# A four-layer graph network on one core: the first group's rows fetched into idle product buffers, and its half blocks projected two at a time amid the first queries

## The chip, the cores and the metric

The kernel runs on one core of a Trainium2 chip. The metric is device time of one execution, in microseconds (us); smaller is better. Before the change it is 3035.61 us, the median of three runs.

## The reference

The input x has 16 graphs of 1024 nodes with 128 features each; one random adjacency matrix (1024 x 1024, about 8 neighbours per node) serves all graphs. Four layers follow one another: L0, L2 and L3 are multi-head attention over neighbours with a feed-forward part, L1 is a graph attention layer. Cut to what matters:

```python
# L0, L2, L3 (8 heads of 16)
Q, K, V = h @ Wq, h @ Wk, h @ Wv
scores = where(adj == 0, -inf, Q K^T / sqrt(16))
x = layer_norm(h + softmax(scores) V @ Wo + bo)
out = layer_norm(x + relu(x @ W1 + b1) @ W2 + b2)
# L1
h = x @ W;  e = leaky_relu(h @ a_src [i] + h @ a_dst [j]), masked by adj
out = layer_norm(softmax(e) h + x)
```

## The kernel before

**Layout.** Nodes are sorted by degree first (the setup, up to about 154 us of the profile), so that a block of 128 sorted nodes has a known bound on neighbours. The 16 graphs are cut into two groups (g) of 8, a group into two halves (h) of 4. There are T = 8 node blocks (t). A *half block* is one (g, t, h): 128 nodes of 4 graphs, 128 x 512 floats, 256 KB.

**Projection.** For every layer and group a table in DRAM holds keys and values of all nodes (1024 rows of 8 KB in attention layers). `project` (L362) takes a half block turned to features x nodes (tile xT): it writes it to DRAM on SP's queue (`kept`, L364), multiplies it with Wkv in two pairs of matmuls (L371), copies each from PSUM to the tile kv on ACT (L375), and writes kv into the table on SP's queue (L380). kv lies in the pool `twos`, which has two buffers for each tag. `turned` (L425) makes xT: four PE transposes (L429) and a copy on ACT (L431). xT has two buffers.

**First layer's input.** `first(g)` (L512) does this for all 16 half blocks of a group: an indirect DMA on POOL's queue gathers the rows in sorted order into the tile xg (L517, one buffer), then come `turned` and `project`. It is a generator: each `yield` ends one step.

**Units.** A unit is one (layer, g, t). Its neighbours come in parts: `gathered` (L581) fetches up to two table rows per node by indirect DMA on POOL (tile e, four buffers, L591), three parts ahead. On DVE, `products` (L597) multiplies them with the queries (L600), `exponentials` (L604) reduces (L614), and ACT takes the exponential (L618); `weighted` (L628) multiplies the values with it (L639), one part later. The products lie in the tile pr, four buffers. `summed` adds them over neighbours on PE (acc, L666). `queries(u)` (L551) needs the unit's x, loaded from `kept` by `loaded(u)` (L540): Wq matmuls (L566), a copy q (L570), replication on PE (L575), copies qr (L578). At the end of a unit `divided` takes the reciprocal (L687), and two tails (`attention_tail`) do the rest of the layer and project for the next one: output projection (L465, L466), norm (L413 and L422 on ACT, L419 on POOL), feed-forward (L479, L483, L488), and again `project`. Unit 0 has ten parts, units 1 to 3 have six each, units 4 to 7 four each, and the same in every group and layer.

**Order.** The order of instructions on each engine is the order in which the program issues them (`manual_schedule`). The main loop goes over all parts of all units. Between the steps of a part `others()` (L713) is called three times: it advances tails, paced over the unit, and then either `fronts` (the next unit's queries) or, where there are none, `slow`:

```python
        if fronts:
            advance(fronts)
        elif slow:
            advance(slow)
```

In an attention part two of these calls stand between the weighted products and the exponentials, and one after the sums; no main work lies between the first two except at a unit's turn. Ahead of the main loop (L723 to L730) `first(0)` is run to its end, x of units 0 and 1 is loaded, and `queries(0)` is run to its end. `first(1)` becomes `slow`: group 1 is projected beside the first units of group 0, a step at a time. It needs three calls for a half block: one for the table write of the half block before, the gather and `turned`, and one for each pair of projections.

Of the kernel before, what the change touches and what calls it, by code (L numbers as in the profile page):

```python
# [12 lines left out]
F32 = mybir.dt.float32  # L13
# [7 lines left out]
P = 128  # L21
D = 128
# [19 lines left out]
T = N // P  # L42
GR = 2
G = B // GR
HF = 2
GH = G // HF
# [30 lines left out]
def sparse_path(ctx: ExitStack, tc: tile.TileContext, a: dict, out: bass.AP, flag):  # L77
# [257 lines left out]
    reps = ctx.enter_context(tc.tile_pool(name="reps", bufs=2))  # L335
    ones_ = ctx.enter_context(tc.tile_pool(name="ones_", bufs=1))
    twos = ctx.enter_context(tc.tile_pool(name="twos", bufs=2))
    smalls = ctx.enter_context(tc.tile_pool(name="smalls", bufs=3))
    exps = ctx.enter_context(tc.tile_pool(name="exps", bufs=2))

    def gather_buffer():
# [17 lines left out]
    srcs = {}  # L359


    def project(l, g, t, h, x):  # L362

        nc.sync.dma_start(kept[l, g][t, :, h, :], x.rearrange("p g n -> p (g n)"))  # L364
        table = tables[l, g][t * P : (t + 1) * P, :]
        if LAYERS[l][1] is ATTN:
            kv = twos.tile([P, 2, GH, D], F32, tag="kv", name="kv")
            for i in range(0, GH, 2):
                ps = bank([P, 2, 2 * D])
                for k in range(2):  # L370
                    nc.tensor.matmul(  # L371
                        ps[:, k, :], x[:, i + k, :], w[LAYERS[l][0], "Wkv"],
                        start=True, stop=True,
                    )
                nc.scalar.copy(  # L375
                    kv[:, :, i : i + 2, :].rearrange("p c g d -> p g c d"),
                    ps.rearrange("p g (c d) -> p g c d", d=D),
                )
                yield
            nc.sync.dma_start(  # L380
                table.rearrange("p (c x) -> p c x", c=2)[:, :, h * GH * D : (h + 1) * GH * D],
                kv.rearrange("p c g d -> p c (g d)"),
            )
            return
        kv = twos.tile([P, GH * D + GH], F32, tag="kv", name="kv")
        if h == 0:
            srcs[g, t] = const.tile([P, G], F32, name=f"src{g}{t}")
        for i in range(0, GH, 2):
            ps = bank([P, 2, D + 2])
            for k in range(2):  # L390
                nc.tensor.matmul(ps[:, k, :], x[:, i + k, :], wg, start=True, stop=True)
            nc.scalar.copy(
                kv[:, i * D : (i + 2) * D].rearrange("p (g d) -> p g d", d=D), ps[:, :, :D]
            )
            to = GH * D + i
            nc.scalar.copy(
                kv[:, to : to + 2].rearrange("p (g o) -> p g o", o=1), ps[:, :, D : D + 1]
            )
            at = h * GH + i
            nc.scalar.copy(  # L400
                srcs[g, t][:, at : at + 2].rearrange("p (g o) -> p g o", o=1), ps[:, :, D + 1 :]
            )
            yield

        nc.sync.dma_start(table[:, h * GH * D : (h + 1) * GH * D], kv[:, : GH * D])
        nc.sync.dma_start(table[:, ROW + h * GH : ROW + (h + 1) * GH], kv[:, GH * D :])
# [18 lines left out]
    def turned(z, dst, gain=None, shift=None):  # L425

        ps = bank([P, GH, P])
        for i in range(GH):
            nc.tensor.transpose(ps[:, i, :], z[:, i, :], ident)  # L429
        if gain is None:  # L430
            nc.scalar.copy(dst, ps)  # L431
        else:
            nc.scalar.activation(dst, ps, AF.Identity, bias=shift, scale=gain)  # L433
# [75 lines left out]
        yield  # L509
        yield from finish(l, g, t, h, z, w["L1", "ln_gamma"], w["L1", "ln_beta"])  # L510

    def first(g):  # L512

        for t in range(T):
            for h in range(HF):
                xg = ones_.tile([P, GH, D], F32, tag="xg", name="xg")
                nc.gpsimd.indirect_dma_start(  # L517
                    out=xg.rearrange("p g d -> p (g d)"), out_offset=None,
                    in_=a["x"].rearrange("n (k c) -> (n k) c", k=GR * HF),
                    in_offset=bass.IndirectOffsetOnAxis(ap=places[:, g, h, t : t + 1], axis=0),  # L520
                )
                xn = states.tile([P, GH, P], F32, tag="xT", name="xT")
                turned(xg, xn)
                yield
                yield from project(0, g, t, h, xn)


    units = [(l, g, t) for l in range(len(LAYERS)) for g in range(GR) for t in range(T)]
# [11 lines left out]
    def loaded(u):  # L540

        if u >= len(units):
            return
        l, g, t = units[u]
        xs[units[u]] = inputs.tile([P, HF, GH, P], F32, tag="x", name="x")
        nc.sync.dma_start(
            xs[units[u]].rearrange("p h g n -> p (h g n)"),
            kept[l, g][t].rearrange("p h c -> p (h c)"),
        )

    def queries(u):  # L551

        l, g, t = units[u]
        if not is_attention(u):
            ps = bank([P, J, G])
            for j in range(J):
                nc.tensor.matmul(ps[:, j, :], rep_of(j, True), srcs[g, t], start=True, stop=True)
            ofs[u] = smalls.tile([P, J, G], F32, tag="of", name="of")
            nc.scalar.copy(ofs[u], ps)
            return  # L560
        qs[u] = reps.tile([P, J, ROW], F32, tag="qr", name="qr")
        for h in range(HF):
            q = ones_.tile([P, GH * D], F32, tag="q", name="q")
            ps = bank([P, GH, D])
            for i in range(GH):
                nc.tensor.matmul(  # L566
                    ps[:, i, :], xs[l, g, t][:, h, i, :], w[LAYERS[l][0], "Wq"],
                    start=True, stop=True,
                )
            nc.scalar.copy(q, ps.rearrange("p g d -> p (g d)"))  # L570
            yield
            pss = []
            for j in range(J):
                ps = bank([P, GH * D])
                nc.tensor.matmul(ps, rep_of(j), q[32 * j : 32 * j + 32], start=True, stop=True)  # L575
                pss.append(ps)
            for j in range(J):
                nc.scalar.copy(qs[u][:, j, h * GH * D : (h + 1) * GH * D], pss[j])  # L578
            yield
# [141 lines left out]
            advance(slow)  # L721

    with tc.manual_schedule():  # L723
        for _ in first(0):
            pass
        loaded(0)
        loaded(1)
        for _ in queries(0):
            pass
        slow.append(first(1))  # L730
        for i in range(AHEAD):
            gathered(i)
        closing = None
        begun = 0
        for i in range(len(parts) + 1):
            here = i < len(parts)
            u = parts[i][0] if here else len(units)
            if here:
                l = units[u][0]
                if i and parts[i - 1][0] != u:  # L740
                    begun = i
                    if units[u][1:] == (0, 1) and l + 1 < len(LAYERS):
                        if LAYERS[l + 1][1] is ATTN:
                            load_weights(LAYERS[l + 1][0])
                if is_attention(u):
                    products(i)
                else:
                    exponentials(i)
            ends = i + 1 >= len(parts) or parts[i + 1][0] != u
            if i:  # L750
                weighted(i - 1, 0)
                if not is_attention(parts[i - 1][0]):
                    others()
                    weighted(i - 1, 2)
                gathered(i - 1 + AHEAD)
            others()
            if closing is not None:
                while tails:
                    advance(tails)
                for _ in closing:  # L760
                    pass
                closing = None
                passes = 3 if is_attention(u) else 4
                steps = STEPS if is_attention(parts[begun - 1][0]) else GRAPH_STEPS
                pace[:] = 0.0, steps / (passes * sum(part[0] == u for part in parts) - 1)
            if here and u + 1 < len(units):
                if i == begun + 1:
                    loaded(u + 2)
                    fronts.append(queries(u + 1))
            others()  # L770
            if here and is_attention(u):
                exponentials(i)
            if i:
                summed(i - 1)
                if parts[i - 1][0] != u:
                    closing = divided(parts[i - 1][0])
                    next(closing)
            others()
            if ends:

                while fronts:
                    advance(fronts)
        while tails:
            advance(tails)
        for _ in closing:
            pass
        while tails:
            advance(tails)
# [434 lines left out]
```

## Time and profile before

| | us |
|---|---|
| median of three runs | 3035.61 (3032.30 to 3037.83) |
| the profiled execution | 3036.25 |
| its span | 3034.5 |
| mean granted PE clock | 0.846 |

| engine | busy us | share of the span |
|---|---|---|
| PE (matmul) | 2124.9 | 70% |
| PEld (weight load) | 1325.2 | 44% |
| DVE | 2150.0 | 71% |
| ACT | 1424.2 | 47% |
| POOL | 1478.1 | 49% |

The DMA queues moved 615 MB, 203 GB/s over the span. The shares are means over stages that differ: the setup with DVE's sorting, the projection of group 0, then 64 units. For a change in one stage the busy time and the waits of that stage count. The time of the profiled execution stands 1.75 us above its span, and 0.64 us above the median.

### The profile page before, as it was taken

The numbers are of one execution on the slowest core, as the hardware profiler recorded it, in microseconds if no ns is written. First come the engines' busy times: TensorE is split into PE (matmuls) and PEld (weight loads), VectorE is DVE, ScalarE is ACT, GpSimd is POOL, SyncE is SP. The second block draws the span as 40 slices with busy tenths as digits, with TensorE's granted clock in tenths as the row PEclk, the third lists the DMA queues.
The fourth block names the chain that finished last, engine by engine and source line by source line (L and its number), as shares of the span: only waits on it lengthen the run. The fifth ranks groups of instructions, "written<-read, shape, count | busy, mean of one in ns | idle before, by whom it ended". The sixth has DMA issues, their size and how long they took to land.

```text
span 3034.5 us, 35305 instructions
## 1 busy us (share of the span) xinstructions
PE 2124.9 (70%) x12569; PEld 1325.2 (44%) x12569; DVE 2150.0 (71%) x1493; ACT 1424.2 (47%) x4468; POOL 1478.1 (49%) x1086
## 2 busy tenths in 40 slices
PE   1365767776777786766577887777877676766766
PEld 1343444543554443434245554555544444334444
DVE  7505768768887666675798767887678877778772
ACT  1033445563556544435345664456543555334454
POOL 0123435443444568685335443354435577466673
PEclk9986888887888888988788988889887888787887
DMA  1057766545555468777665654656546553355540
GB/s 56 12 181 287 304 215 236 204 169 217 223 225 179 171 210 288 256 272 282 221 238 216 228 205 179 271 218 230 200 183 245 198 216 145 144 219 210 195 144 22
DMA packets 171144, 615.36 MB, mean 203 GB/s; under 512 B 44472, under 2 KB 47928, under 8 KB 122462
## 3 DMA queue, kind: packets, MB, share of 16 engines
q0 software_dynamic: 99584, 480.93, 43.4%
q1 hardware_dynamic: 71376, 132.10, 11.9%
q8 instruction: 101, 1.65, 0.2%
q14 instruction: 83, 0.68, 0.1%
HBM read 650.67 MB, written 100.73 MB: 248 GB/s over the span
## 4 chain that ended last, share of the span: by engine, by line
PE 40%; DVE 15%; ACT 14%; POOL 11%; issue 10%; DMA 8%; another core or an unknown queue 0%; SPq 0%; POOLq 0%; DVEq 0%; ACTq 0%
PE ps L479 7%; PE yps L488 6%; PE ps L429 5%; ACT z L413 5%; POOL e L591 5%; PE acc L666 5%; POOL rstd L419 4%; DVE sc L614 4%; DMA xg<-in_x,places 3%; DVE pr L639 3%; PE ps L371 3%; DVE pr L600 3%; ACT qr L578 3%; PE yps L465 3%; PE yps L492 3%
## 5 line engine op out<-in xcount | busy, mean ns | idle before, releaser
L591 POOL DMA_INDIRECT e<-table,idx x656 | 886.1, 1351 | 448.1 <-DVE pr L639 263.4
L639 DVE TENSOR_TENSOR pr<-e,ex 128x2048 f32<-128x2048 f32 (+1 forms) x344 | 760.1, 2216 | 338.7 <-ACT ex L618 333.4
L419 POOL TENSOR_TENSOR rstd<-total,power 128x4 f32<-128x4 f32 x224 | 359.9, 1608 | 753.4 <-ACT z L413 718.9
L600 DVE TENSOR_TENSOR pr<-e,qr 128x2048 f32<-128x2048 f32 (+1 forms) x258 | 565.1, 2190 | 195.1 <-ACT qr L578 138.1
L666 PE MATMUL acc<-pr,marks 128*32 128x512 f32 x2624 | 467.7, 701 | 146.5 <-DVE pr L639 136.6
L614 DVE TENSOR_REDUCE sc<-pr 128x128 f32<-128x2048 f32 (+1 forms) x258 | 561.9, 2178 | 0.0
L429 PE MATMUL ps<-ident,z 128*128 128x128 f32 x768 | 199.4, 368 | 246.5 <-ACT z L422 246.5
L429 PEld LDWEIGHTS ps<-ident,z 128*128 128x128 f32 x768 | 126.5, 172 | 396.2 <-ACT z L422 325.7
L371 PE MATMUL ps<-Wkv,xT 128*128 128x256 f32 x768 | 244.5, 466 | 41.5 <-ACT xT L431 21.2
L479 PE MATMUL ps<-x,W 128*128 128x512 f32 x384 | 241.1, 761 | 41.8 <-ACT x L433 41.8
L488 PE MATMUL yps<-W,f 128*128 128x128 f32 x1536 | 258.5, 287 | 13.0 <-ACT f L483 11.0
L666 PEld LDWEIGHTS acc<-pr,marks 128*32 128x32 f32 x2624 | 89.4, 120 | 398.5 <-issue 213.8
L488 PEld LDWEIGHTS yps<-W,f 128*128 128x128 f32 x1536 | 212.5, 197 | 69.9 <-ACT f L483 44.3
L483 ACT ACTIVATE f<-ps,b 128x512 f32<-128x512 f32 x192 | 131.4, 687 | 230.8 <-PE ps L479 230.0
L578 ACT COPY qr<-ps 128x512 f32<-128x512 f32 x384 | 197.6, 596 | 74.9 <-PE ps L575 74.7
L413 ACT ACTIVATE z<-y,root 128x128 f32<-128x128 f32 x512 | 198.5, 396 | 50.6 <-DVE y L506 35.4
L575 PE MATMUL ps<-q,rep 32*128 32x512 f32 x768 | 169.7, 679 | 67.4 <-ACT oT L431 41.3
L371 PEld LDWEIGHTS ps<-Wkv,xT 128*128 128x128 f32 x768 | 166.2, 231 | 91.2 <-ACT xT L431 29.3
L618 ACT ACTIVATE ex<-sc 128x128 f32<-128x128 f32 (+1 forms) x258 | 81.1, 314 | 253.6 <-DVE sc L614 236.1
L465 PE MATMUL yps<-Wo,oT 128*128 128x128 f32 x768 | 180.2, 322 | 7.5 <-ACT oT L431 6.9
L375 ACT COPY kv<-ps 128x512 f32<-128x512 f32 x192 | 112.5, 587 | 140.9 <-PE ps L371 129.4
L413 ACT ACTIVATE z<-yps,root 128x128 f32<-128x128 f32 x384 | 135.6, 368 | 77.2 <-PE yps L492 77.2
(128 smaller groups left out, 2977.8 us busy)
## 6 DMA issues: line engine op xcount, KB each, us to landing
table<-kv SPq DMA_DIRECT2D x96, 512.0 KB
kept<-xT SPq DMA_DIRECT2D x128, 256.0 KB
x<-kept SPq DMA_DIRECT2D x64, 512.0 KB
e<-table,idx POOLq DMA_INDIRECT x656
table<-kv SPq DMA_DIRECT2D x32, 256.0 KB
edges<-in_adj SPq DMA_DIRECT2D x8, 512.0 KB
W<-in_L_gnn_W SPq DMA_DIRECT2D x6, 128.0 KB
xg<-in_x,places POOLq DMA_INDIRECT x32
```

The lines of the kernel that those rows point to most:

```text
L371: nc.tensor.matmul(ps[:, k, :], x[:, i + k, :], w[LAYERS[l][0], "Wkv"], start=True, stop=True,)
L413: nc.scalar.activation(z[:, i, :], y[:, i, :], AF.Square, scale=D**-0.5, bias=root, accum_out=total[:, i : i + 1],)
L419: nc.gpsimd.tensor_tensor(rstd, total, power, ALU.pow)
L429: nc.tensor.transpose(ps[:, i, :], z[:, i, :], ident)
L479: nc.tensor.matmul(ps, p["W1"][:, f * P : (f + 1) * P], x1.rearrange("p g n -> p (g n)"), start=True, stop=True,)
L488: nc.tensor.matmul(ps[:, i, :], f1[:, f, i * P : (i + 1) * P], p["W2"][:, f, :], start=(f == 0), stop=False,)
L578: nc.scalar.copy(qs[u][:, j, h * GH * D : (h + 1) * GH * D], pss[j])
L591: nc.gpsimd.indirect_dma_start(out=es[i][:, k, :], out_offset=None, in_=tables[l, g][:, :], in_offset=bass.IndirectOffsetOnAxis(ap=idx[:, ...
L600: nc.vector.tensor_tensor(prs[i][0][:, :n, :], es[i][:, :n, :ROW], qs[u][:, j : j + n, :], ALU.mult)
L614: nc.vector.tensor_reduce(sc[:, :n, :], prs[i][0][:, :n, :].rearrange("p k (a d) -> p k a d", d=HD), mybir.AxisListType.X, ALU.add,)
L639: nc.vector.tensor_tensor(prs[i][k0 // 2][:, :m, :].rearrange("p k (a d) -> p k a d", d=d), es[i][:, k0 : k0 + m, base : base + ROW].rearr ...
L666: nc.tensor.matmul(accums[u][32 * j : 32 * j + 32, h, :], marks[:, CHUNK[t, r, j], :], tiles[j // 2][:, j % 2, h * GH * D : (h + 1) * GH * D],
```

## The change

Ahead of the main loop stands `at_once(0)`. It gathers the half blocks of group 0 into the buffers of pr, two half blocks to a buffer, four buffers: up to eight half blocks are on their way before the first is turned. After the gathers of every two node blocks the half blocks in hand are advanced two at a time, a step each. When the first two blocks are begun, x of unit 0 is loaded and `queries(0)` joins the generators that are advanced in turn. x of unit 1 is loaded at the end.

Group 1 stays in `slow`, as `at_leisure(1)`. A half block there is now four steps: gather; `turned`; one pair of projections; the other. The table write falls into the same step as the next gather. Its xg and its kv have the same tag "io" in the pool `ones_`, which has one buffer for each tag: the two take turns in it. kv of the tails stays in `twos`.

The pool `smalls` (sc, total, rstd, both, of) has two buffers for each tag instead of three. In the changed file the lines from L513 on lie lower: the gather of xg is L514, e is gathered in L619.

```diff
-    smalls = ctx.enter_context(tc.tile_pool(name="smalls", bufs=3))
+    smalls = ctx.enter_context(tc.tile_pool(name="smalls", bufs=2))
...
-    def project(l, g, t, h, x):
+    def project(l, g, t, h, x, pool=None):
...
-            kv = twos.tile([P, 2, GH, D], F32, tag="kv", name="kv")
+            kv = (pool or twos).tile([P, 2, GH, D], F32, tag="io" if pool else "kv", name="kv")
...
-    def first(g):
-
+    def first(g, t, h, xg, pool=None):
+
+        nc.gpsimd.indirect_dma_start(
+            out=xg.rearrange("p g d -> p (g d)"), out_offset=None,
+            in_=a["x"].rearrange("n (k c) -> (n k) c", k=GR * HF),
+            in_offset=bass.IndirectOffsetOnAxis(ap=places[:, g, h, t : t + 1], axis=0),
+        )
+        yield
+        xn = states.tile([P, GH, P], F32, tag="xT", name="xT")
+        turned(xg, xn)
+        yield
+        yield from project(0, g, t, h, xn, pool)
+
+    def at_leisure(g):
         for t in range(T):
             for h in range(HF):
-                xg = ones_.tile([P, GH, D], F32, tag="xg", name="xg")
-                nc.gpsimd.indirect_dma_start(
...
+                yield from first(
+                    g, t, h, ones_.tile([P, GH, D], F32, tag="io", name="xg"), ones_
                 )
-                xn = states.tile([P, GH, P], F32, tag="xT", name="xT")
-                turned(xg, xn)
-                yield
-                yield from project(0, g, t, h, xn)
+
+    def at_once(g):
+
+
+        todo, now = [], []
+        for t in range(T):
+            xg = prods.tile([P, HF, GH, D], F32, tag="pr", name="xg")
+            for h in range(HF):
+                gen = first(g, t, h, xg[:, h])
+                next(gen)
+                todo.append(gen)
+            if len(todo) < 4:
+                continue
+            while todo:
+                while todo and len(now) < 2:
+                    now.append(todo.pop(0))
+                advance(now)
+            if t == 1:
+                loaded(0)
+                now.append(queries(0))
+        while now:
+            advance(now)
+        loaded(1)
...
-        for _ in first(0):
-            pass
-        loaded(0)
-        loaded(1)
-        for _ in queries(0):
-            pass
-        slow.append(first(1))
+        at_once(0)
+        slow.append(at_leisure(1))
```

More of the change, by code (lines that the diff above doesn't have):

```diff
@@ L510, in graph_tail @@
         yield from finish(l, g, t, h, z, w["L1", "ln_gamma"], w["L1", "ln_beta"])
-    def first(g):
+    def first(g, t, h, xg, pool=None):
[10 more added lines that the diff above has]
+    def at_leisure(g):
         for t in range(T):
             for h in range(HF):
-                xg = ones_.tile([P, GH, D], F32, tag="xg", name="xg")
-                nc.gpsimd.indirect_dma_start(
-                    out=xg.rearrange("p g d -> p (g d)"), out_offset=None,
-                    in_=a["x"].rearrange("n (k c) -> (n k) c", k=GR * HF),
-                    in_offset=bass.IndirectOffsetOnAxis(ap=places[:, g, h, t : t + 1], axis=0),
-                )
-                xn = states.tile([P, GH, P], F32, tag="xT", name="xT")
-                turned(xg, xn)
-                yield
-                yield from project(0, g, t, h, xn)
+                yield from first(
+                    g, t, h, ones_.tile([P, GH, D], F32, tag="io", name="xg"), ones_
+                )
+    def at_once(g):
[18 more added lines that the diff above has]
+        loaded(1)
     units = [(l, g, t) for l in range(len(LAYERS)) for g in range(GR) for t in range(T)]
```

## The prediction

> **What bounds the kernel now.** I read the page for the shape of the time, then busy time by stage, then the chain of waits and the timeline of the two stages that the diff touches. Bounds of the units are the starts of DVE's reciprocal (L687: 340.4, 410.5, 466.2, 513.5 us), so the stages below are: projection of group 0, hand-over, units 0 to 3 of layer 0 (group 1 is projected beside them), and, for comparison, a unit with six parts and no such work beside it (751.1 on). Columns: stretch, its length, busy time of PE, PEld, DVE, ACT and POOL, PE clock, DMA share, GB/s.
>
> ```profile
> 154.50:240.90 86.40, 59.89 (x194) 41.89 (x194) 0.16 (x1) 28.14 (x48) 16.56 (x16) 0.80 0.54 185
> 240.90:258.20 17.30, 8.30 (x32) 4.60 (x32) 0.02 (x1) 4.36 (x9) 8.93 (x9) 0.59 0.92 344
> 258.20:340.40 82.20, 50.00 (x242) 28.11 (x242) 65.95 (x34) 24.59 (x51) 32.84 (x26) 0.77 0.81 307
> 340.40:410.50 70.10, 47.00 (x287) 33.56 (x288) 43.24 (x24) 31.92 (x97) 23.65 (x22) 0.83 0.73 274
> 410.50:466.20 55.70, 41.36 (x271) 28.52 (x270) 42.96 (x24) 30.72 (x99) 25.71 (x19) 0.87 0.56 190
> 466.20:513.50 47.30, 36.09 (x218) 23.02 (x218) 39.88 (x24) 25.65 (x85) 21.46 (x17) 0.82 0.58 217
> ...
> 751.10:800.50 49.40, 39.67 (x232) 25.07 (x232) 42.94 (x25) 25.70 (x88) 22.43 (x17) 0.79 0.57 213
> ```
>
> In the first stage DVE is idle and nothing is full: a latency bound. Units 1 and 2 take 70 and 56 us for the DVE work (43 us) that takes 49 us elsewhere. The chain of waits in the first stage repeats one pattern, ten times:
>
> ```profile
> 177.14 4.51 DMA xg<-in_x,places
> 181.65 0.14 issue
> 181.79 0.64 PE ps L429 x4
> ```
>
> One xg buffer: gather, transposes (L429), next gather; 5.3 us a half block (154.7 to 234.65 in 15 steps), projection hidden inside it. For group 1 the timeline shows the same line of work at two PE speeds, and what a late gather does:
>
> ```profile
> 265.33 1.09 PE L429 MATMUL ps<-ident,xg 128*128 128x128 f32 x4 [8.28 <-DMA xg<-in_x,places]
> ...
> 310.89 0.66 PE L429 MATMUL ps<-ident,xg 128*128 128x128 f32 x4
> ...
> 390.79 1.11 PE L429 MATMUL ps<-ident,xg 128*128 128x128 f32 x4 [6.28 <-DMA xg<-in_x,places]
> ...
> 392.42 0.31 ACT L618 ACTIVATE ex<-sc 128x128 f32<-128x128 f32 x1
> ...
> 392.76 2.29 DVE L639 TENSOR_TENSOR pr<-e,ex 128x2048 f32<-128x2048 f32 x1 [7.02 <-ACT ex L618]
> ...
> 401.01 0.52 SPq L380 DMA_DIRECT2D table<-kv  x1
> ...
> 407.10 0.37 ACT L392 COPY kv<-ps 128x256 f32<-128x256 f32 x1 [5.71 <-DMA table<-kv]
> ```
>
> PE waits 6.28 us for rows of group 1, the exponential stands behind their copy on ACT, and DVE loses 7.02 us. Over units 0 to 3 DVE loses so to late exponentials:
>
> ```profile
> DVE pr L639 <- ACT ex L618: 56.2, 19, 8.9
> ```
>
> [...]a 256 KB gather takes 3.7 to 4.7 us to reach PE, a 512 KB table write 4.4 us (issued 240.85, the waiting gather starts 245.22) to 6.1 us (401.01 to 407.10). [...]transposes 1.09 us after 8.28 us idle, 0.66 us otherwise; the four projections after them 3.78 and 1.99 us.
>
> **The change part by part.**
>
> *Projection of group 0: a gain.* Eight gathers start at once into four idle product buffers, four more products' worth follow as transposes free them; POOL spends 1.0 us each, beside the weight loads. The rows are there before PE starts at 154.5 (xg issued from about 133 to 151, landing 4 us later), so the 4.5 us DMA link leaves the loop. Next late: PE's own line. Transposes 0.64, copy and hand-over 0.7, projections 2.0, hand-over 0.1: 3.45 us a half block at full clock. Two others lie close: two kv buffers, each busy from its first copy to its write's landing (1.7 + 5.2 = 6.9 us for two halves: 3.5 each), and traffic of 1.05 MB a half block at the 344 GB/s of the second row: 3.05 us. I take 3.9 us (3.45 to 4.6). The first four half blocks are interleaved and carry queries(0): their copies, matmuls and the load of x, which stands on SP between table writes. Cold PE (3.8 us per half), the wait for two table writes, and some 8 us for 8 qr and 2 q copies make that 25 us, to 179.5 (before: 176.2, without queries). Behind them queries leave two generators out of step, so the other twelve go one after the other: last transposes at 179.5 + 11 x 3.9 = 222.4 instead of 234.65, and from there to the last table write 4 us warm instead of 6.2: 14.5 us earlier. Hand-over: 245.22 to 258.18, of which queries(0) were the end; an estimate for the two e gathers of the first part is 2.1 MB at 344 GB/s, 6.1[...]; I take 3.5. **Sum: -18 us (-10 to -22).**
>
> *Smaller edits.* smalls from 3 to 2: sc, total, rstd, both and of are each rewritten two uses later, after readers that DVE or the tails must pass anyway (weighted(i) stands behind exp(i), all tails end before the next closing): 0. POOL's memset of e (14 us) moves behind the eight gathers: its users come at 225, cover 60 us. `loaded(1)` moves behind all table writes: used a unit later. Leisure's kv leaves the pool of the tails: takes away waits like the 5.71 us above, at most two or three seen: inside the range.
>
> *Group 1 beside units 0 to 3: a loss.* Before, a half block takes three calls of others(): gather with transposes, then two projections; a gather needs only the last transposes, so it runs ahead on POOL. After, xg and kv share **one** buffer "io". So gather k+1 waits on POOL until the table write of half k has landed, and the transposes come one call later: four calls. This is a closed loop on in-order engines:
> - transposes to issue of the table write: 6.2 us cold (265.33 to 271.53), 4.0 warm (310.89 to 314.90). PE idles 9 us in each loop, so cold: 6.2;
> - landing of the write: 5.2 (4.4 to 6.1);
> - gather to transposes: 4.2 (3.7 to 4.7); POOL's e gathers have drained while it stood;
> - acc matmuls (L666, 3.03 us cold) lie inside in two of three phases: 2.0.
>
> Together **17.6 us** in unit 0. Before, it was 82.2 us over some ten half blocks there, 8.2 each. In units 1 to 3 tails run on PE too; L465, L479 and L488 alone are 680 us over 48 attention units, 14 us each, with transposes and centre about 24 over 18 calls: 1.3 each, two calls in the loop: 20.2 us. Four calls equal 1.33 parts, 8.8 us of DVE's work (3 x 2.2 each), so the loop sets the pace wherever slow work is advanced.
> Unit 0, from the first e gather: transposes 1 at 20 us as before; queries take five calls, which hide one round, transposes 2 at 38; then 17.6 each, the sixth at 108; its projections and exponential end the unit at 115. Before: 332.4 - 245.2 = 87. **+28.**
> Units 1 to 3: 13 calls each are left by the queries, 3.25 half blocks x 20.2 = 66 us; three make 198 against 70.1 + 55.7 + 47.3 = 173. **+25.** Calls in all: 30 + 3 x 18 less 4 x 5 = 64, just the 16 x 4 needed, so unit 4 (41 us) stays as it is.
> Queued behind the waiting gather on POOL: e gathers of parts two ahead (over 20 us of slack at that pace, so 0) and rstd of the tails, which ACT waits for: not shown before in this form; 0 to 5 us for each of 12, I take 0, the upper end goes into the range. The loss may be nil or less: with a warm PE, 4.4 and 3.9 us the loop is 12.3 us, units 1 to 3 then run at 49.4 and unit 0 at some +6.
>
> **Sum:** 3036.25 - 18 + 53 = **3071 us** (the profiled execution's own time; its span 3034.5 plus 1.75; 0.6 above the median 3035.61).
>
> **The rivals.**
> 1. Forecast, loop about 15.5 to 21 us: 3045 to 3115. For it: every link is measured in this trace. Chance 0.60.
> 2. *The gain stands alone* (faster): the loop is short or its waits fall under DVE's work. One us of loop is worth 4 us in unit 0 and 3 x 3.25 in units 1 to 3, 13.75; so 35 us are gone when it is 2.5 us shorter: below **15.1 us** in unit 0 it is faster. At 12.3: -18 + 6 - 25 = -37, 2999; at 14: about 3020. For it: the warm rows at 310.89, fewer half blocks per unit, kv out of the tails' way.[...] 0.17.
> 3. *POOL as a second bound*: rstd behind waiting gathers, 12 x 3 to 5 us on top: 3107 to 3130. For it: POOL's order; against: tails have slack of a unit. 0.16.
> 4. *The two cancel*, or half blocks still wait for a kv buffer as long as for xg before: 3030 to 3042. 0.07.
>
> That nothing changes is no case: in the first stage nothing else covers the gather.
>
> **How the numbers follow.** Likeliest: 3071. The range 3012 to 3116 takes most of 1, 4, half of 2 and the start of 3. A measurement of this kernel tells about 0.2%, 6 us, from no change: faster 0.17, same 0.07, slower 0.76.
>
> **What would show it.** In the changed profile: PE's first transposes follow each other at about 4 us, no gather in the chain there; products start about 240 instead of 258; then L514 on POOL idle until "DMA table<-kv" some 5 us each, PE waiting 8 us and more for xg, the first reciprocal some 113 us after the first product, the next three 66 us apart (82, 70, 56 and 47 before). Wrong, if units 0 to 3 take no more than 260 us from the first product, or if the first stage is no shorter than 76 us.

## The result and the profile after

The changed kernel takes **3068.26 us** (median of 4 runs, 3064.21 to 3072.41) against 3033.95 for the kernel before, run beside it (4 runs, 3027.94 to 3037.83): ratio **1.0115** [1.0092, 1.0138], +34.3 us. In a later comparison it came to 1.0147 [1.0126, 1.0169], 3063.69 us against 3021.44. The forecast was 3071, +35. The profiled execution took 3072.41 us, its span 3070.6. The kernel before took 3034 us in the first comparison and 3020.5 to 3021.4 us in the later ones, these each on a chip of its own, so only ratios and differences within one comparison are compared below.

First the busy time by stage: projection of group 0 with queries(0), hand-over, units 0 to 3, cut as for the kernel before at the starts of the first product and of the reciprocals (354.28, 420.02, 491.52, 560.61 us). Columns as before: stretch, length, busy time of PE, PEld, DVE, ACT and POOL, PE clock, DMA share, GB/s.

```profile
163.20:227.40 64.20, 47.77 (x225) 36.62 (x225) 0.16 (x1) 32.02 (x58) 7.56 (x8) 0.97 0.65 229
227.40:241.00 13.60, 0.00 (x0) 0.00 (x0) 0.04 (x1) 0.00 (x0) 6.93 (x8) 0.57 0.78 277
241.00:354.30 113.30, 52.12 (x216) 27.46 (x217) 66.20 (x35) 19.33 (x42) 30.40 (x25) 0.65 0.60 218
354.30:420.00 65.70, 43.97 (x272) 29.48 (x270) 43.03 (x23) 30.70 (x95) 24.19 (x18) 0.82 0.64 232
420.00:491.50 71.50, 44.06 (x264) 30.50 (x264) 43.26 (x24) 30.35 (x96) 24.60 (x22) 0.83 0.58 207
491.50:560.60 69.10, 47.37 (x265) 32.52 (x266) 40.14 (x23) 30.77 (x96) 23.65 (x20) 0.73 0.59 206
```

The first stage has shrunk and holds the queries' PE work as well. DVE's busy time in units 0 to 3 is what it was; the units have grown to 113.3, 65.7, 71.5 and 69.1 us, 319.6 in all, from 82.2, 70.1, 55.7 and 47.3, 255.3 in all. In unit 0 PE is busy 46% of the time (52.12 of 113.3 us) instead of 61% (50.00 of 82.2), and the DMA share is 0.60 instead of 0.81: both have more gaps there than before. PE's granted clock was 0.65 there (0.77 before), the memory traffic 218 GB/s (307 before).

The chain of waits of the first stage, where a DMA of xg stood at each step, now reads so (start, duration, what):

```profile
199.35 5.72 DMA kept<-xT
205.16 0.59 ACT xT L431
...
205.80 2.01 PE ps L371 x8
207.83 0.44 ACT kv L375
208.31 0.60 ACT xT L431
208.92 0.04 issue
208.96 2.01 PE ps L371 x8
```

No gather is left in it. From one projection to the next it is PE and ACT, 3.16 us a half block. From 193 us to the last table write it passes twice through a write whose buffer the next copy needs: this one of xT (5.72 us), and at 217.92 us a table write (5.01 us). These writes take hardly longer than the line of PE and ACT beside them: the step that ends with the first lasts 3.38 us, the one around the second 3.16. Over the whole stage ACT's copies into kv waited for table writes four times, 5.9 us in all.

For group 1 the timeline of one turn of the loop:

```profile
310.03 0.52 SPq L380 DMA_DIRECT2D table<-kv  x1
...
313.85 0.96 POOL L514 DMA_INDIRECT xg<-in_x,places  x1 [11.81 <-DMA table<-kv]
...
317.37 1.08 PE L429 MATMUL ps<-ident,xg 128*128 128x128 f32 x4 [7.99 <-DMA xg<-in_x,places]
...
318.49 0.58 ACT L431 COPY xT<-ps 128x512 f32<-128x512 f32 x1 [8.48 <-PE ps L429]
318.97 0.26 ACT L646 ACTIVATE ex<-sc 128x64 f32<-128x64 f32 x1
319.26 1.23 DVE L667 TENSOR_TENSOR pr<-e,ex 128x1024 f32<-128x1024 f32 x1 [8.64 <-ACT ex L646]
...
323.55 0.52 SPq L380 DMA_DIRECT2D table<-kv  x1
...
327.63 1.48 POOL L514 DMA_INDIRECT xg<-in_x,places  x1 [10.24 <-DMA table<-kv]
```

Read it link by link: write issued 310.03, landed and gather issued 313.85 (3.8 us), rows at PE 317.37 (3.5), next write 323.55 (6.2), gather 327.63 (4.1). The exponential, whose scores DVE had reduced by 309.48, stands on ACT behind the copy of xT, which waits for the transposes, which wait for the gather, which waits for the write; so DVE loses 8.64 us in this one turn. In totals (engine, instruction and releaser: us waited, times, longest; POOL and PE over 240 to 560 us, DVE over units 0 to 3):

```profile
POOL xg L514 <- DMA table<-kv: 112.7, 11, 14.5
```

```profile
PE ps L429 <- DMA xg<-in_x,places: 115.4, 15, 24.8
```

```profile
DVE pr L667 <- ACT ex L646: 118.6, 22, 11.8
```

Four more waits of these gathers, 25.0 us, are put down to acc, z and f by the profile; they too ended 3.85 to 3.87 us after a table write was issued, so they most likely belong here. DVE's wait for late exponentials was 56.2 us in 19 waits; it grew by 62.4 us, and the four units by 64.3 us.

### The profile page after: what moved, and what is told of

The parts are those of the page before. It is cut to its first block, busy times and chain, and to the rows that moved or that the text cites. A ratio compares the mean times of both kernels' runs of the same rounds, so it can differ in the third digit from the quotient of the medians.

```text
span 3070.6 us, 35347 instructions
## 1 busy us (share of the span) xinstructions
PE 2111.8 (69%) x12569; PEld 1318.5 (43%) x12569; DVE 2156.2 (70%) x1493; ACT 1421.1 (46%) x4468; POOL 1463.7 (48%) x1086
## 3 DMA queue, kind: packets, MB, share of 16 engines
q1 hardware_dynamic: 71376, 132.10, 11.7%
## 4 chain that ended last, share of the span: by engine, by line
PE 39%; ACT 15%; DVE 12%; POOL 11%; issue 9%; DMA 8%; POOLq 0%; DVEq 0%; SPq 0%; ACTq 0%
PE ps L479 7%; PE yps L488 5%; ACT z L413 5%; PE ps L429 5%; POOL e L619 5%; PE acc L694 5%; POOL rstd L419 4%; PE ps L371 4%; DVE sc L642 4%; DVE pr L667 3%; DVE pr L628 3%; ACT qr L606 3%; PE yps L465 3%; PE ps L603 3%; PE yps L492 3%
## 5 line engine op out<-in xcount | busy, mean ns | idle before, releaser
L619 POOL DMA_INDIRECT e<-table,idx x656 | 871.4, 1328 | 459.3 <-DVE pr L667 254.4
L429 PEld LDWEIGHTS ps<-ident,z 128*128 128x128 f32 x768 | 125.8, 170 | 388.3 <-ACT z L422 316.4
L371 PE MATMUL ps<-Wkv,xT 128*128 128x256 f32 x768 | 231.9, 445 | 37.3 <-ACT xT L431 18.7
L488 PEld LDWEIGHTS yps<-W,f 128*128 128x128 f32 x1536 | 212.8, 197 | 69.3 <-ACT f L483 42.9
L371 PEld LDWEIGHTS ps<-Wkv,xT 128*128 128x128 f32 x768 | 157.9, 220 | 85.0 <-ACT xT L431 25.9
L514 POOL DMA_INDIRECT xg<-in_x,places x32 | 39.8, 1243 | 303.5 <-DVE low L211 131.9
L422 ACT ACTIVATE z<-y,rstd 128x128 f32<-128x128 f32 x512 | 162.6, 392 | 25.4 <-POOL rstd L419 25.2
```

Source lines behind the costliest of these rows:

```text
L371: nc.tensor.matmul(ps[:, k, :], x[:, i + k, :], w[LAYERS[l][0], "Wkv"], start=True, stop=True,)
L488: nc.tensor.matmul(ps[:, i, :], f1[:, f, i * P : (i + 1) * P], p["W2"][:, f, :], start=(f == 0), stop=False,)
L619: nc.gpsimd.indirect_dma_start(out=es[i][:, k, :], out_offset=None, in_=tables[l, g][:, :], in_offset=bass.IndirectOffsetOnAxis(ap=idx[:, ...
```

## The experiments

**The theory.** There are two parts of opposite sign: the fetch at once takes some 17 us off the start, and the buffer that group 1's rows and values share adds some 50 to 60 in units 0 to 3. **Rivals:** the loss comes from the fourth step of a half block rather than from the buffer; it comes from the start itself (queries amid projections, products' buffers taken); or from POOL's order, where rstd of the tails stands behind waiting gathers.

*e1_once_only: the first part alone.* Group 1 as it was: rows in their own buffer, values from `twos`, gather and transposes in one step.

```diff
-                yield from first(
-                    g, t, h, ones_.tile([P, GH, D], F32, tag="io", name="xg"), ones_
-                )
+                gen = first(g, t, h, ones_.tile([P, GH, D], F32, tag="xg", name="xg"))
+                next(gen)
+                yield from gen
```

> Group 0 as in the changed kernel, group 1 as before (xg and kv in buffers of their own, gather and transposes in one call). If the loss comes from the one buffer that group 1's rows and keys share, only the gain of the first stage is left: about 17 us below the kernel before, 3017 (3010 to 3024), units 0 to 3 together about 255 us from the first product. If the new order of the first stage or the smaller pool costs time later on, it stays above 3040.

Measured: 3008.13 us against 3020.5, ratio **0.9957** [0.9942, 0.9972], 12.4 us faster, where some 17 were expected (10 to 24). The first product starts at 240.32 us; units 0 to 3 take 85.5, 72.7, 55.9 and 47.4 us, 261.5 in all (about 255 were expected). DVE's and POOL's waits over these units:

```profile
DVE pr L667 <- ACT ex L646: 61.4, 19, 9.2
```

```profile
POOL xg L514 <- PE ps L429: 34.5, 9, 7.5
```

The gather waits for transposes again and no longer for a write, and DVE's wait is back near the 56 us of before. The early start costs the units little (6 us of its 18).

*e2_leisure_only: the second part alone.* Group 0 one half block after the other, then the queries, as before; group 1 as in the change.

```diff
-        at_once(0)
+        for t in range(T):
+            for h in range(HF):
+                for _ in first(0, t, h, ones_.tile([P, GH, D], F32, tag="io", name="xg")):
+                    pass
+        loaded(0)
+        loaded(1)
+        for _ in queries(0):
+            pass
```

> Group 0 as before, group 1 as in the changed kernel (one buffer for rows and keys, four calls). If the loss lies here, it is the slowest of all: 3034 + 50 to 64, so 3084 to 3098, with POOL waiting for table writes some 110 us in units 0 to 3. If the loss came with the first stage, it stays near 3034.

Measured: 3077.4 us against 3020.5, **1.0194** [1.0167, 1.0221], 56.9 us slower. First product at 258.77, units 107.0, 64.2, 69.7 and 66.4 us (307.4). The loop's wait is there without any early start:

```profile
POOL xg L514 <- DMA table<-kv: 119.8, 12, 14.7
```

-12.4 and +56.9 make 44.5; the change as a whole measured +34.3 in one comparison and +42.3 in another. So the two parts account for it to within 2 to 10 us, and the start is not the source of the loss.

*e6_three_calls: the buffer or the fourth step?* The changed kernel with gather and transposes in one step, so three steps a half block, the shared buffer kept.

```diff
-                yield from first(
-                    g, t, h, ones_.tile([P, GH, D], F32, tag="io", name="xg"), ones_
-                )
+                gen = first(
+                    g, t, h, ones_.tile([P, GH, D], F32, tag="io", name="xg"), ones_
+                )
+                next(gen)
+                yield from gen
```

> The changed kernel with gather and transposes of group 1 in one call again, so three calls for a half block, but rows and keys still in one buffer. If the closed loop of write, landing, gather and transposes is the cause, it is still there, only crowded into fewer units: 3055 (3040 to 3070). If the fourth call is the cause, about 3020.

Measured: 3092.64 us against 3020.5, **1.0245** [1.0221, 1.0269], 72.1 us slower. Units 144.4, 87.5, 62.0 and 48.5 us (342.4). The expected size was missed, and on the other side of the changed kernel: fewer steps are worse. DVE's wait in its units 0 to 3:

```profile
DVE pr L669 <- ACT ex L648: 143.0, 23, 12.3
```

Its loop is as long as in the changed kernel: seven turns from the gather at 287.25 us to that at 386.33 take 14.2 us each, against 14.3. But three steps are one part, so each part lasts a whole loop; with four steps the loop spreads over 1.33 parts, 10.8 us each. The units agree: the ten parts of unit 0 take 14.4 us each here (144.4 us) and 11.3 in the changed kernel. With the shared buffer, then, the fourth step is a relief and not the loss. Against e1, which has the same three steps and differs only in the buffers, the medians stand 84.5 us apart, and these belong to the shared buffer. What four steps cost with buffers of their own is not known: e3_own_buffers, which has them, gave no time, since its instructions wait for one another in a circle.

*e4_smalls_two: the small pool alone.* The kernel before, with that pool at two buffers.

```diff
-    smalls = ctx.enter_context(tc.tile_pool(name="smalls", bufs=3))
+    smalls = ctx.enter_context(tc.tile_pool(name="smalls", bufs=2))
```

> The kernel before with two instead of three buffers in the pool smalls. By the forecast nothing waits for these buffers: ratio 1.000 (0.998 to 1.002). If a third buffer mattered, slower by more than 0.3%.

Measured: 3023.17 against 3021.07 us, **1.0008** [0.9994, 1.0022]: no difference that can be told, as the forecast had it.

*e5_late_memset: where the start lost 8.5 us.* The profile after holds one thing that the prediction did not have. PE's first transposes start at 163.24, not at 154.7, although the rows are there. In the timeline:

```profile
147.87 13.99 POOL L346 MEMSET e<- 128x4128 f32 x4
...
153.28 8.60 DVE L260 TENSOR_SCALAR mean<-mean 128x2 f32<-128x2 f32 x1
153.36 8.53 DVE L308 TENSOR_TENSOR ln_b<-ln_b,b 128x1 f32<-128x1 f32 x1
...
163.24 1.95 PE L429 MATMUL ps<-ident,xg 128*128 128x128 f32 x8
```

Two elementwise instructions of DVE on one or two columns last 8.6 us and end with POOL's memsets, four back to back (the second probably only stands behind the first); behind them on DVE stands wgT, for which PE's instruction ahead of the transposes waits (from 154.5 to 162.79). In the kernel before, the memsets stood 5 us earlier, and the same instruction lasted 3.44 us, to 153.37, the end of the third of the four:

```profile
142.85 13.99 POOL L346 MEMSET e<- 128x4128 f32 x4 [8.26 <-issue]
...
149.93 3.44 DVE L260 TENSOR_SCALAR mean<-mean 128x2 f32<-128x2 f32 x1
```

The experiment moves the memset behind `at_once(0)`:

```diff
-    for _ in range(AHEAD + 1):
-        nc.gpsimd.memset(gather_buffer(), 0.0)
-
...
         at_once(0)
+        for _ in range(AHEAD + 1):
+            nc.gpsimd.memset(gather_buffer(), 0.0)
```

> The changed kernel, with POOL's four memsets of the buffers e behind the sixteen gathers of group 0 instead of ahead of the last eight. In the changed kernel PE began its transposes 8.5 us later than before, with two small DVE instructions drawn out until the memsets' end. If the memsets hold DVE up, the first transposes come at about 155 instead of 163.2 and the whole is 8 us shorter than the changed kernel: ratio to before about 1.009 instead of 1.0115. If the eight gathers themselves delay the weights (DMA traffic), the start stays near 163 and the ratio at 1.0115.

Measured: 3056.67 us against 3021.07, 1.0123 [1.0103, 1.0142]. The timeline:

```profile
153.67 0.17 DVE L260 TENSOR_SCALAR mean<-mean 128x2 f32<-128x2 f32 x1
153.75 0.16 DVE L308 TENSOR_TENSOR ln_b<-ln_b,b 128x1 f32<-128x1 f32 x1
...
192.94 13.99 POOL L751 MEMSET e<- 128x4128 f32 x4
```

The same two take 0.17 us, PE's transposes start at 155.73 and the first product at 232.77 instead of 240.96. So the memset's place was the cause, and 8 us come back at the first product. The ratio does not show them (1.009 was expected). Whether they reach the end is not settled: run again beside the changed kernel on one chip (f2_late_memset_again and f1_changed_again), the medians are 4.9 us apart, and the intervals of the two ratios overlap.

> The changed kernel itself once more, beside the next two: 1.0115 times the kernel before, as in the first comparison (1.009 to 1.014).

> e5_late_memset once more, on one chip with the changed kernel. Its profile has the first product 8.2 us earlier than the changed kernel's, its ratio (1.0123) doesn't show it. If the 8 us last to the end, it stands 0.27% below f1_changed_again; if they are given back in units 0 to 3 or later, the two are equal.

Measured: 1.0147 [1.0126, 1.0169] for the changed kernel, just above the range expected, and 1.0129 [1.0110, 1.0148] with the late memset.

*e8_once_late_memset: e1 and the late memset together.*

> e1_once_only with the memsets behind the gathers. If memsets and group 1's buffer add up, it is 8 us below e1_once_only: ratio about 0.993. If the first stage's end is set by something else (table writes landing), it stays at 0.9957.

Measured: 3003.97 us against 3021.07, 0.9938 [0.9921, 0.9955]; first product at 234.37, units 84.9, 72.6, 55.8 and 47.4 us. With group 1 as before the gain of the start stands, 17 us. The ratio is 0.19% below that of e1, as far as two comparisons with overlapping intervals can tell.

*e7_one_ahead: the buffer opened instead of shared.* As e8, and the next half block's rows are fetched as soon as the transposes have read the current ones, a step or more ahead. The first fetch also moves ahead of the first gathers of e.

```diff
-        for t in range(T):
-            for h in range(HF):
-                yield from first(
-                    g, t, h, ones_.tile([P, GH, D], F32, tag="io", name="xg"), ones_
-                )
+        halves = [(t, h) for t in range(T) for h in range(HF)]
+        def fetched(t, h):
+            gen = first(g, t, h, ones_.tile([P, GH, D], F32, tag="xg", name="xg"))
+            next(gen)
+            return gen
+        coming = fetched(*halves[0])
+        yield
+        for n in range(len(halves)):
+            gen = coming
+            next(gen)
+            if n + 1 < len(halves):
+                coming = fetched(*halves[n + 1])
+            yield
+            yield from gen
...
         slow.append(at_leisure(1))
+        advance(slow)
```

> e8_once_late_memset, with the gather of group 1's next half block issued right behind the transposes of the one before (three calls a half block, own buffer for rows), and its first gather ahead of the gathers of e. If the wait of PE for rows is what DVE loses in units 0 to 2, PE's 67 us of waiting for rows falls below 20 and DVE's 61 us behind late exponentials to about 35: ratio about 0.985. If these exponentials are late for other reasons (tails, keys' buffers), it stays near 0.993.

Measured: 2984.54 us against 3021.07, **0.9879** [0.9863, 0.9896], 36.5 us faster than before. Units 83.4, 66.6, 48.2 and 48.9 us (247.2). DVE's and PE's waits in it (its lines are numbered differently):

```profile
DVE pr L675 <- ACT ex L654: 40.0, 14, 14.2
```

```profile
PE ps L426 <- DMA xg<-in_x,places: 31.9, 5, 22.4
```

PE waits for rows 5 times instead of 15 in the changed kernel, and DVE less than in the kernel before. The expectation was a little too good: PE's wait was to fall below 20 us and the ratio to about 0.985; 22.4 of the 31.9 us are the wait for the very first rows. This version is faster than both. Its two edits, the fetch ahead and the earlier first fetch, were not tried apart.

> e7_one_ahead once more: 0.988 times the kernel before (0.986 to 0.990), about 2.4% below the changed kernel on the same chip.

Measured again, beside f1 and f2: 0.9881 [0.9860, 0.9902].

**The account closes in units 0 to 3.** The shift of the last reciprocal of these four units (513.53 us in the profile of the kernel before) against the measured difference of medians:

| kernel | first product, us | units 0 to 3, us | shift of unit 3's end | measured |
|---|---|---|---|---|
| changed | 240.96 | 319.6 | +47.1 | +34.3 |
| changed again | 240.11 | 315.4 | +42.0 | +42.3 |
| once only | 240.32 | 261.5 | -11.7 | -12.4 |
| leisure only | 258.77 | 307.4 | +52.6 | +56.9 |
| three calls | 240.83 | 342.4 | +69.7 | +72.1 |
| late memset | 232.77 | 313.9 | +33.1 | +35.6 |
| once, late memset | 234.37 | 260.7 | -18.4 | -17.1 |
| one ahead | 233.03 | 247.2 | -33.3 | -36.5 |
| small pool alone | 260.27 | 257.1 | +3.9 | +2.1 |
| late memset again | 233.31 | 316.4 | +36.2 | +37.4 |
| one ahead again | 233.32 | 243.6 | -36.6 | -36.2 |

What happens by the end of unit 3 is, within 5 us, what is measured at the end. The one exception is the changed kernel's first comparison, by 13 us; the second fits. Behind unit 3 the profile of the kernel before still lasts 2521.0 us, the longest of all; those of the changed kernel last 2510.0 and 2500.5, and that with the small pool alone, whose time is that of the kernel before, 2507.2. So the profiles give no sign of a gain later in the kernel; why the first comparison comes out smaller stays open.

## Why the prediction was right, and where its steps were off

The signs, the mechanism of the loop and the order of the stages came as forecast. That the sum lies within 3 us of the first measurement is in part luck: errors of opposite sign stand in both halves of it.

**The projection of group 0.** Forecast -18 us at the first product, measured -17.2 (240.96 against 258.18). Two errors cancel in it.
- *"The rows are there before PE starts at 154.5"* was right for the rows and wrong for the start: 163.24. The step that failed is *"POOL's memset of e (14 us) moves behind the eight gathers: its users come at 225, cover 60 us"*. It looked at who reads the memset's result and not at who runs beside it: DVE's last setup instructions, and PE behind them. In the trace the first of these lasts from 153.28 to 161.88 us; two memsets of 3.55 us that began meanwhile still went first, and it ended with the last of them. That it is the memset was shown (0.17 us without it, e5); by what means it holds DVE up was not.
- *Half block 3.9 us*: it is 3.16, below the lower end of 3.45. The 0.6 us of the transposes do not lengthen the line, since PE runs them while ACT still copies the last projections to kv (194.78 to 195.38 us, for one). The bound of the two kv buffers, which lay close, hardly showed: kv's copies waited for table writes twice in these eleven steps, 2.9 us in all. Eleven steps took 35.6 us instead of 42.9.
- The first four with the queries took 24.6 us (forecast 25); last transposes 223.42 (222.4); from the first e gather to the first product 9.0 us, 4.0 less than the 13.0 before (forecast 3.5 less, an estimate of the author's).

**The loop of group 1.** The mechanism was right; it is what e2 and e6 against e1 show. Its terms:

| term | forecast, us | measured, us |
|---|---|---|
| landing of the write | 5.2 | 3.8 to 4.5, once 12.4 |
| gather to transposes | 4.2 | 3.4 to 4.1 |
| transposes to write, acc included | 6.2 + 2.0 | 6.2 to 8.7 |
| loop in unit 0 | 17.6 | 14.3 (mean of five) |
| loop in units 1 to 3 | 20.2 | 21.8 (mean of nine, with the queries) |

The first three rows are unit 0's. The landing was taken from two writes, of 4.4 and 6.1 us; most turns came out below both, and why was not tested. In units 1 to 3 it was 3.8 to 3.9 us in six turns and 6.4, 7.5 and 9.9 us in three. The slow transposes with which the loop was reckoned came: 1.08 to 1.12 us in the six turns from 273.71 to 346.98 us, at a granted clock of 0.50, behind 6.0 to 8.5 us in which PE was idle.

**Unit 0: right by two errors.** With 14.3 us the prediction's own break-even (15.1 in unit 0) would have said faster, rival 2. It didn't come, because unit 0 is more than the turns of the loop. Transposes 2 came 42 us after the first e gather (forecast 38): the write of half 1 took 12.4 us to land, 257.59 to 270.01, amid the e gathers. The sixth came at 99.8 instead of 108, and the last weighted product at 106 instead of 115. But then the seventh half block's transposes stand ahead of unit 1's first exponential, and DVE takes the weighted product that needs it before unit 0's reciprocal: 354.28, 16 us after the last weighted product of unit 0. So 113.3 us, where 113 were named. The break-even was the weak step: it let one loop length stand for unit 0 and, scaled, for units 1 to 3, and they parted: 3.3 us shorter than forecast in the one, 1.6 longer in the others, while unit 0 gave its gain back to the seventh half block.

**Units 1 to 3.** 66 each was forecast, 65.7, 71.5 and 69.1 came: 206.3 in all, 8 more than the 198. The mis-sized term is the loop: 20.2 us was forecast, 21.8 measured. Fewer turns than the 9.75 of the forecast fall there, nine from the gather at 341.72 us to the last at 537.55; the last table write is issued at 549.91, 10.7 us ahead of unit 3's reciprocal.

**The sum.** The 28 us of unit 0 run from the first e gather and so already hold the shorter hand-over of 3.5 us, which the -18 counts again; without that the forecast is +38.5. The profile has +47 at unit 3's end, the two comparisons +34 and +42.

**The rivals.** *The gain stands alone* is refuted by e2. *POOL as a second bound*: no. Over units 0 to 3 ACT waited for rstd 0.8 us in all (0.2 before), and DVE, behind its first product, 1.3 us for rows of e. *Half blocks still wait for a kv buffer* in group 0: hardly, four waits and 5.9 us in all.

The sign of POOL's idle time was as said, its size not: 10 us a gather rather than 5, as the count starts when POOL runs out of other work and not when the write is issued. PE's wait for rows is 7.7 us in the mean, 6.5 without the first of 24.8.

## What to carry to other kernels

A buffer that takes the input of a step and the output of the same step in turn joins the end of one round to the start of the next: write landing, gather, compute, all in series (3.8, 3.5 and 6.2 us in the turn shown), and here that cost 57 us alone (e2). The early fetch of group 0 with separate buffers for group 1 gained 12 us (e1), 17 with the memset moved as well (e8), and 36 with group 1's rows fetched one step ahead besides (e7). When work is moved on an engine's queue, ask not only who needs its result but what runs beside its new place, also on engines that it has no data in common with (here a DVE instruction of 0.17 us lasted 8.60 beside POOL's memsets). When side work sets the pace, count its steps per unit of main work: a step more can be a relief, as it spreads a wait over more of the work that hides it (10.8 us a part instead of 14.2 here).

## What was not expected of the hardware

A DVE instruction of 0.17 us on 128 x 2 values lasted 3.44 and 8.60 us beside POOL's memsets, in the second case to the end of the last of four. Two of the four began while it stood (at 154.8 and 158.3 us), and the change from one to the next did not let it in. In the kernel before it did: there the instruction ended with the third memset, and the next ones of DVE ran at their usual length beside the fourth (0.43 us on 128 x 256 at 153.40). The same operation on 128 x 1 values was not held up in either kernel (two of them in 0.27 us, at 147.84 before and at 150.61 after). What decides was not tested.

A 512 KB table write landed in 3.8 to 4.5 us in most turns of the loop in unit 0, in 4.5 us ahead of the first e gather, and in 12.4 us once, amid e gathers (353 GB/s from 257.6 to 270 us). It is no accident of one execution: the same write took 9.7 us in f1_changed_again, 10.7 in e5_late_memset and 13.0 in f2_late_memset_again. In e6_three_calls, where no e gather was issued from 244 us until behind the gather that waits for it, it took 4.3 us. The load of x stands elsewhere there too, so the e gathers are the likely cause and not a shown one.
